# A bitonic sort beside graph layer 0: operand and mask of the compare-exchange held in PSUM

## The chip, the cores and the metric

The kernel runs on one core of a Trainium2 chip. The metric is the device time of one execution in microseconds. A core has TensorE (PE, with its weight loads PEld), VectorE (DVE), ScalarE (ACT), GpSimd (POOL) and SyncE (SP), which run side by side and wait for each other by semaphores. In this kernel POOL's main task is to issue gathers: DMAs that fetch 128 rows of a table by a list of indices.

## The reference

Four graph layers over 12500 nodes of 128 features and 200000 edges, each behind a layer norm with ReLU. Only layer 0 and the edge list of layer 1 bear on the change.

```python
edge_index = jnp.stack([src, dst])
h = jnp.maximum(_layernorm(x, axis=-1), 0.0)
x = x + _L0_gnn_ref(h, edge_index, edge_attr_64, ...)     # attention over incoming edges, sums by dst
h = jnp.maximum(_layernorm(x, axis=-1), 0.0)
x = x + _L1_gnn_ref(h, edge_attr_3, edge_weight1, ..., edge_index)   # attention, sums by src
...                                                        # layers 2 and 3

# layer 0
h = x @ W
a_s = h @ att_src
a_d = h @ att_dst
e = jax.nn.leaky_relu(a_s[src] + a_d[dst], NEG_SLOPE)
e = jnp.exp(e - seg_max[dst])
denom = jax.ops.segment_sum(e, dst, num_segments=N)
alpha = e / (denom[dst] + 1e-16)
out = jax.ops.segment_sum(h[src] * alpha[:, None], dst, num_segments=N)
```

Layer 0 sums over edges in the order of dst, in which the edges arrive. Layer 1 sums over edges in the order of src, so the kernel has to sort the edges by src first, and to carry edge_weight1 along.

## The kernel before, in words

**Layer 0's edges** (`layer0_edges`) go by in NW = 391 groups of G = 4 tiles of 128 edges. For each group POOL issues four gathers (line 289) that fetch 128 rows each of the table hw into the tile rows, of which there are eight buffers. SP loads a row of lanes. DVE turns lanes into a one-hot matrix (mine, L1116), PE multiplies it (pt, L1119), and DVE makes the edge weights from pt and the gathered rows (L1122 to L1130). ACT makes three of the four weight matrices (L1137, L1138), DVE the fourth (L1140). PE multiplies them by the rows (psum, L1143), and DVE adds the product to acc (L1146, two instructions per group).

**The sort** (`sort`, given out by `background`) runs in the same stretch of the program. After 8 of every 15 groups `layer0_edges` takes one step of it. The 200000 keys lie in a tile of 128 partitions with 13 x 128 elements each, and edge_weight1 in another of this shape, aux. A step is either a transposition of keys and aux (`turn`: PE multiplies by an identity or a diagonal matrix into the PSUM tile bank, of which there are two buffers, and ACT copies out; L459 to L470), or one compare-exchange of all pairs at a distance (`exchange`). Levels 1 to 6 treat the pairs in two pieces of 416 each, one upwards and one downwards, and the other levels mostly in one piece of 832 or 800. There are 171 exchanges with 194 pieces.

A piece has first operands a and second operands b, strided views of keys. Before the change:

- L427, DVE: mask = a > b (or a < b), into a contiguous SBUF tile mask
- L428, ACT: copies the first half of the pairs of aux into the SBUF tile swap
- L431 and L432, DVE: minimum and maximum of a and b into the other keys tile
- L437 and L438, DVE, once all pieces have had these: conditional copies within aux, the second half where mask is set into the first, and swap where mask is set into the second.

**Order.** The program is written in the order above; a scheduler of the framework then interleaves the instructions of groups and sort steps in each engine's queue, by its own costs. Each engine runs its queue in order. A tile with several buffers is written again when the readers of its last use are done.

Of the kernel before, what the change touches and what calls it, by code (L numbers as in the profile page):

```python
# [23 lines left out]
F32 = mybir.dt.float32  # L24
# [3 lines left out]
AF = mybir.ActivationFunctionType  # L28
# [8 lines left out]
P = 128  # L37
# [9 lines left out]
RC = -(-R // P)  # L47
# [57 lines left out]
class Net:  # L105
    def __init__(self, tc, a, out):
        self.tc, self.nc, self.a, self.out = tc, tc.nc, a, out

# [14 lines left out]

    def bank(self, psum):

        return psum.tile([P, 512], F32, name="bank", bufs=2)

    def constants(self, pool, temp, psum):  # L130
        nc, a = self.nc, self.a
# [263 lines left out]
    def sort(self, work, psum, keys, aux=None):  # L395

        nc = self.nc  # L400
        at, ax = 0, 0

        def flat(t):
            return t.rearrange("p c e -> p (c e)")

        def exchange(pieces, rest=(), both=True):


            nonlocal at
            k, o = flat(keys[at]), flat(keys[1 - at])  # L410
            if aux:
                mask = work.tile([P, RC * P // 2], F32, name="mask")
                swap = work.tile([P, RC * P // 2], F32, name="swap")
                v = flat(aux[ax])
            used = 0
            swaps = []
            for va, vb, up in pieces:
                a, b = va(k), vb(k)
                shape = list(a.shape[1:])
                n = int(np.prod(shape))  # L420
                if aux:
                    m, s = (t[:, used:used + n] for t in (mask, swap))
                    if len(shape) > 1:
                        names = "abc"[:len(shape)]
                        spec = f"p ({' '.join(names)}) -> p {' '.join(names)}"
                        m, s = (t.rearrange(spec, **dict(zip(names, shape))) for t in (m, s))
                    nc.vector.tensor_tensor(m, a, b, op=OP.is_gt if up else OP.is_lt)  # L427
                    nc.scalar.activation(s, va(v), AF.Copy)  # L428
                    swaps.append((va(v), vb(v), m, s))
                    used += n  # L430
                nc.vector.tensor_tensor(va(o), a, b, op=OP.min if up else OP.max)  # L431
                nc.vector.tensor_tensor(vb(o), a, b, op=OP.max if up else OP.min)  # L432
            for lo, hi in rest:
                nc.scalar.activation(o[:, lo:hi], k[:, lo:hi], AF.Copy)
            for a, b, m, s in swaps:
                m = m.bitcast(I32)
                nc.vector.copy_predicated(a, m, b)  # L437
                nc.vector.copy_predicated(b, m, s)  # L438
            at = 1 - at

        def halves(lo, hi, d):
            def view(h):
                return lambda t: t[:, lo:hi].rearrange("p (a h d) -> p a h d", h=2, d=d)[:, :, h, :]
            return view(0), view(1)

        def span(lo, n, to):
            return lambda t: t[:, lo:lo + n], lambda t: t[:, to:to + n]

        def turn(dst, src, level):

            for c0 in range(0, RC, 4):
                n = min(4, RC - c0)
                p = self.bank(psum).rearrange("p (c e) -> p c e", e=P)
                rows = P if c0 + n < RC else R - (RC - 1) * P
                for j in range(n):
                    c = c0 + j
                    cols = flat(src)[:, c * P:c * P + rows]
                    if level is None:
                        nc.tensor.transpose(p[:rows, j, :], cols, self.ident)  # L459
                    elif level == 0:  # L460
                        nc.tensor.transpose(p[:, j, :rows], src[:rows, c, :], self.ident[:rows, :rows])
                    else:
                        d = self.level_diag(c, level)
                        nc.tensor.matmul(p[:, j, :rows], src[:rows, c, :], d[:rows, :rows], start=True, stop=True)
                if level is None:
                    nc.scalar.activation(dst[:rows, c0:c0 + n, :], p[:rows, :n, :], AF.Copy)
                elif rows == P:
                    nc.scalar.activation(dst[:, c0:c0 + n, :], p[:, :n, :], AF.Copy)
                else:
                    nc.scalar.activation(flat(dst)[:, c0 * P:c0 * P + rows], p[:, 0, :rows], AF.Copy)  # L470

        def turn_all(level):
            nonlocal at, ax
            turn(keys[1 - at], keys[at], level)
            at = 1 - at
            if aux:
                turn(aux[1 - ax], aux[ax], None if level is None else 0)
                ax = 1 - ax


        for level in range(1, 8):
            for e in range(level - 1, -1, -1):
                d = 1 << e
                if level == 7:
                    exchange([(*halves(0, RC * P, d), True)])
                else:
                    size = 1 << level

                    def view(r, h, size=size, d=d):
                        return lambda t: t.rearrange("p (a r m h d) -> p a r m h d", r=2, m=size // (2 * d), h=2,  # L490
                                                     d=d)[:, :, r, :, h, :]
                    exchange([(view(0, 0), view(0, 1), False), (view(1, 0), view(1, 1), True)])
                yield None
        for level in range(8, 19):
            turn_all(level)
            yield None
            d = 1 << (level - 8)
            cols = R
            while d:
                if d < 64:  # L500
                    exchange([(*halves(0, cols, d), True)])
                elif d < 512:
                    exchange([(*halves(0, 24 * 64, d), True)], rest=[(24 * 64, cols)])
                elif d == 512:
                    exchange([(*span(0, 512, 512), True), (*span(1024, 64, 1536), True)], rest=[(1088, 1536)])
                else:
                    exchange([(*span(0, 576, 1024), True)], rest=[(576, 1024)])
                yield None
                d //= 2
            turn_all(None)  # L510
            yield None
            for e in range(6, -1, -1):
                exchange([(*halves(0, RC * P, 1 << e), True)])
                yield None
        yield keys[at], aux[ax] if aux else None
# [584 lines left out]
    def layer0_edges(self, acc, lists, tb, background):  # L1100
        nc, tc = self.nc, self.tc
        idx, place, half, mask, firsts = lists
        n = D + 2
        with tc.tile_pool(name="l02", bufs=1) as work, tc.tile_pool(name="ps02", bufs=2, space=PSUM) as psum:
            steps = background(psum)
            for g in range(NW):
                lo = g * G
# [13 lines left out]
                t = work.tile([P, G, 2, 3], F32, name="factor", bufs=2)  # L1121
# [19 lines left out]
                p = psum.tile([P, n], F32, name="psum", bufs=2)  # L1141
# [6 lines left out]
                    next(steps, None)  # L1148
            for _ in steps:
                pass  # L1150

    def layer0_wide(self, pool, acc, asd, least, wide, edges):

# [743 lines left out]
```

## Time and profile before

| | |
|---|---|
| median of 3 runs | 9236.6 us (9233.54 to 9252.93) |
| profiled execution, its own time | 9221.37 us |
| profiled execution, span from first to last instruction | 9219.6 us |
| first and last gather of hw | 177.5 and 2428.0 us from the span's start |
| busy in the span: PE, DVE, ACT, POOL | 6457.1, 6759.6, 4358.4, 5288.2 us |

The span is the time from the first instruction to the last. The profiled execution is 1.8 us longer than its span and 15.2 us shorter than the median of the runs. The busy time of an engine is the union of its instructions; a part of the kernel is read from its own stretch, not from these sums. In a group's row the number after the bar is the busy time, then the mean of one instruction in ns, then the engine's idle time just before them and what ended it.

### The profile page before, as it was taken

To read this page: it belongs to the slowest core of one execution; us is meant where nothing else is said; L and a number is where in the kernel's file an instruction comes from. 1 tells how busy PE (TensorE), PEld (TensorE's weight loads), DVE (VectorE), ACT (ScalarE), POOL (GpSimd) and SP (SyncE) were. 2 spreads that over 40 slices of the span, in tenths; PEclk is the share of its full clock that TensorE was granted. 3 is DMA by queue.
4 is the path that set the end of the run, shared out by engine and by line. 5 is a ranking of instruction groups with operands and counts; after the bars stand their busy time and mean duration, and the time that the engine had idled before them with its cause. 6 is when DMAs were issued, how large, how long until landed. Compare 5 with 4: busy or idle time off the path is not lost. (4 is left out here: it accounts for less than half of the span.)

```text
span 9219.6 us, 138919 instructions
## 1 busy us (share of the span) xinstructions
PE 6457.1 (70%) x35725; PEld 4629.3 (50%) x35726; DVE 6759.6 (73%) x24903; ACT 4358.4 (47%) x7941; POOL 5288.2 (57%) x5216
## 2 busy tenths in 40 slices
PE   4454545544456777777777638887888876999999
PEld 3344444444335777677667524444444433555555
DVE  5777677767656777877777787777777776777777
ACT  4444444444333555555565443333333335655555
POOL 1777777777535666567666457777777771000000
PEclk7555555555565555555555559999999997999999
DMA  4233333333464555455555413433444443233333
GB/s 111 72 71 71 69 71 72 70 70 71 129 190 145 166 163 162 139 155 162 159 161 161 121 56 111 117 114 109 116 117 117 112 121 101 87 99 97 98 97 111
DMA packets 916156, 1046.92 MB, mean 114 GB/s; under 512 B 136970, under 2 KB 754595, under 8 KB 914593
## 3 DMA queue, kind: packets, MB, share of 16 engines
q1 hardware_dynamic: 698837, 557.92, 21.7%
q0 software_dynamic: 185408, 438.42, 17.4%
q10 hardware_dynamic: 31115, 41.46, 1.5%
q8 instruction: 319, 5.23, 0.2%
q14 instruction: 477, 3.90, 0.1%
HBM read 977.06 MB, written 86.50 MB: 115 GB/s over the span
## 5 line engine op out<-in xcount | busy, mean ns | idle before, releaser
L849 PE MATMUL sums<-yours,r 128*128 128x482 f16 x10192 | 2535.5, 373 | 192.8 <-ACT r L875 149.5
L875 ACT ACTIVATE r<-pout 128x512 f16<-128x512 f32 x2548 | 1480.0, 596 | 1940.4 <-PE pout L870 1914.2
L289 POOL DMA_INDIRECT rows<-hw,idxd x1564 | 1773.0, 1134 | 653.4 <-issue 390.0
L289 POOL DMA_INDIRECT rows<-kvt,idxs x1660 | 1600.0, 964 | 852.0 <-issue 399.0
L872 DVE TENSOR_SCALAR yours<-iotac,bucketp 128x482 f16<-128x482 f16 x5096 | 1642.1, 358 | 387.2 <-PE sums L849 386.5
L289 POOL DMA_INDIRECT rows<-zt,idxs x1660 | 1614.8, 973 | 509.9 <-issue 403.5
L849 PEld LDWEIGHTS <-r 128*128 128x128 f16 x10192 | 970.7, 99 | 988.7 <-ACT r L875 349.4
L1143 PE MATMUL psum<-rows,weights 128*128 128x130 f32 x3128 | 812.1, 435 | 703.5 <-ACT weights L1138 651.0
L1143 PEld LDWEIGHTS psum<-rows,weights 128*128 128x128 f32 x3128 | 690.1, 321 | 785.4 <-ACT weights L1138 744.3
L1317 PE MATMUL psum<-weighted,hot 128*128 128x137 f32 x3320 | 843.6, 432 | 252.1 <-DVE lg L1294 93.0
L870 PE MATMUL pout<-z,mine 128*128 128x256 f16 x5096 | 928.3, 277 | 11.1 <-DVE mine L864 8.9
L1317 PEld LDWEIGHTS psum<-weighted,hot 128*128 128x128 f32 x3320 | 741.0, 316 | 302.1 <-ACT weighted L1307 144.5
L1138 ACT ACTIVATE weights<-off,weight,minus 128x128 f32<-128x128 bf16 x1173 | 496.8, 482 | 833.3 <-DVE rows L1130 741.3
L1463 DVE TENSOR_TENSOR acc<-acc,psum 128x128 f32 x1660 | 464.6, 280 | 488.3 <-PE psum L1459 482.9
L1289 PE MATMUL pb<-we,near 128*128 128x8 f32 x3320 | 688.5, 336 | 165.1 <-PE psum L1317 91.7
L1289 PEld LDWEIGHTS pb<-we,near 128*128 128x128 f32 x3320 | 683.5, 304 | 222.4 <-PE psum L1317 128.3
L1286 ACT ACT_TABLE_LOAD x370 | 474.7, 1283 | 638.5 <-DMA near<-lengths 635.5
L870 PEld LDWEIGHTS <-mine 128*128 128x128 f16 x5096 | 479.1, 98 | 452.5 <-DVE mine L864 51.1
L1319 DVE TENSOR_TENSOR acc<-acc,psum 128x137 f32 x1660 | 488.5, 294 | 225.7 <-PE psum L1317 218.5
L1282 PE MATMUL pq<-q,mine 128*128 x3320 | 460.3, 286 | 230.1 <-DVE mine L1278 122.4
L1307 ACT ACT_TABLE_LOAD x370 | 474.7, 1283 | 309.9 <-DVE lg L1302 269.9
L1282 PEld LDWEIGHTS <-mine 128*128 128x128 f16 x3320 | 368.6, 133 | 286.2 <-issue 123.0
(455 smaller groups left out, 9490.8 us busy)
## 6 DMA issues: line engine op xcount, KB each, us to landing
lanes<-lanes SPq DMA_DIRECT2D x168, 896.0 KB
near<-lengths SPq DMA_DIRECT2D x415, 256.0 KB
lanes<-slanes SPq DMA_DIRECT2D x415, 128.0 KB
lanes<-dlanes SPq DMA_DIRECT2D x391, 128.0 KB
z<-zt SPq DMA_DIRECT2D x98, 448.0 KB
z<-h SPq DMA_DIRECT2D x98, 448.0 KB
rows<-kvt,idxs POOLq DMA_INDIRECT x1660
rows<-zt,idxs POOLq DMA_INDIRECT x1660
```

The source lines that it names most:

```text
L289: self.nc.gpsimd.indirect_dma_start(out=out, out_offset=None, in_=table, in_offset=bass.IndirectOffsetOnAxis(ap=idx[:, t:t + 1], axis=0))
L849: nc.tensor.matmul(sums[i], self.part(r[:, i, :], h), yours[:, i, :], start=s == 0 and h == 0, stop=s == NB - 1 and h == PARTS - 1)
L870: nc.tensor.matmul(p[:, j, :], mine[:, (i + j) * P:(i + j + 1) * P], z[:, s % ZB, :], start=True, stop=True)
L872: nc.vector.tensor_scalar(yours[:, j, :], self.iotac, place[:, b:b + 1], None, op0=OP.is_equal)
L875: nc.scalar.activation(r, p, AF.Copy)
L1138: nc.scalar.activation(hot[:, j, :], off, AF.Relu, bias=w[:, j:j + 1], scale=minus[:, j:j + 1])
L1143: nc.tensor.matmul(p, hot[:, j, :], rows[:, j, :n], start=j == 0, stop=j == G - 1)
L1282: nc.tensor.matmul(pq[:, j, :], mine[:, j, :], q[:, bass.ds(blocks[j], 1), h, :].rearrange("p a d -> p (a d)"), start=h == 0, stop=h == 1)
L1286: nc.scalar.activation(hid, hid, AF.Silu, bias=self.be1, scale=self.we1)
L1289: nc.tensor.matmul(pb[:, j, :], hid[:, j, :], self.we2, start=True, stop=True)
L1317: nc.tensor.matmul(p, hot, v[:, j, :], start=True, stop=True)
L1319: nc.vector.tensor_add(d, d, p)
```

## The change

In an exchange that carries aux, the mask is no longer a tile in SBUF. mask and a new tile first are the two buffers of bank in PSUM. ScalarE copies the first operand a of each piece into first, in contiguous order, and DVE reads first wherever it read a: for the comparison, the minimum and the maximum. The conditional copies read the mask from PSUM. The second operand b, aux and swap stay in SBUF. For the length of `layer0_edges` a buffer of bank is two PSUM banks wide (1024 elements of fp32), so that a piece of 832 fits; `turn` uses the first 512 elements of it.

```diff
@@ class Net, __init__
+        self.banks = 1
@@ def bank(self, psum)
-        return psum.tile([P, 512], F32, name="bank", bufs=2)
+        return psum.tile([P, 512 * self.banks], F32, name="bank", bufs=2)
@@ def sort, exchange
             if aux:
-                mask = work.tile([P, RC * P // 2], F32, name="mask")
+                mask, first = self.bank(psum), self.bank(psum)
                 swap = work.tile([P, RC * P // 2], F32, name="swap")
                 v = flat(aux[ax])
...
                 if aux:
-                    m, s = (t[:, used:used + n] for t in (mask, swap))
+                    m, s, f = (t[:, used:used + n] for t in (mask, swap, first))
                     if len(shape) > 1:
...
-                        m, s = (t.rearrange(spec, **dict(zip(names, shape))) for t in (m, s))
+                        m, s, f = (t.rearrange(spec, **dict(zip(names, shape))) for t in (m, s, f))
+                    nc.scalar.activation(f, a, AF.Copy)
+                    a = f
                     nc.vector.tensor_tensor(m, a, b, op=OP.is_gt if up else OP.is_lt)
                     nc.scalar.activation(s, va(v), AF.Copy)
@@ def sort, turn
-                p = self.bank(psum).rearrange("p (c e) -> p c e", e=P)
+                p = self.bank(psum)[:, :512].rearrange("p (c e) -> p c e", e=P)
@@ def layer0_edges
+            self.banks = 2
             steps = background(psum)
...
             for _ in steps:
                 pass
+            self.banks = 1
```

The sort before layer 0, which runs only where the edges do not come in order, carries no aux and is left as it is.

## The prediction

> **What bounds the kernel now.** I read the page first, for where the sort beside layer 0 lies: the slices in which POOL shows 7 and DVE 5 to 8, from 177 to 2428 us. Then the busy time of each engine in that stretch, the groups of POOL, and the waits.
>
> ```profile
> 177.00:2428.00 2251.00, 1093.46 (x5398) 938.68 (x5397) 1590.84 (x4910) 1056.63 (x2728) 1773.16 (x1565) 0.55 0.31 73
> ```
>
> ```profile
> L289 POOL DMA_INDIRECT rows<-hw,idxd x1564 | 1773.0, 1134 | 653.4 <-issue 390.0 <-ACT off L1137 176.0 <-DMA rows<-hw,idxd 34.3
> ```
>
> The first view's columns are PE, PEld, DVE, ACT, POOL. No engine looks full; POOL comes nearest with 1773 of 2251 us. The group's row tells why it is the bound all the same: of its idle time 176 us lie before the first gather. Read one by one, the 1564 gathers run from 177.5 to 2428.0 us with a gap of 0.303 to 0.306 us between each two of nearly all (477.6 us in 1563 gaps; two exceed 0.4 us). POOL never stands for a buffer. So the stage lasts as long as the gathers: 1773 + 478 = 2251 us.
>
> The waits of this stretch show the others following:
>
> ```profile
> DVE weight L1125 <- DMA rows<-hw,idxd: 350.0, 175, 10.4
> ACT swap L428 <- DVE aux L438: 207.2, 78, 8.4
> ...
> DVE factor L1122 <- PE pt L1119: 143.6, 162, 2.0
> DVE acc L1146 <- PE psum L1143: 111.9, 155, 1.4
> ```
>
> DVE stands 350 us until gathered rows land. The other large DVE waits, 143.6 + 111.9 = 255 us, are for PE.
>
> Next, why a gather takes 1134 ns on average. Half of them take 940 to 945 ns, the longest 2597. The timeline shows which are long:
>
> ```profile
> 1005.64 1.01 DVE L427 TENSOR_TENSOR mask<-keys 128x832 f32<-128x832 f32 x1
> ...
> 1005.83 1.64 POOL L289 DMA_INDIRECT rows<-hw,idxd  x1 [0.30 <-issue]
> ...
> 1017.24 1.01 DVE L431 TENSOR_TENSOR keys<-keys 128x832 f32<-128x832 f32 x1
> 1017.31 1.76 POOL L289 DMA_INDIRECT rows<-hw,idxd  x1 [0.30 <-issue]
> ```
>
> A gather that starts while a sort instruction runs ends 0.82 us after that instruction ends (1006.65 + 0.82 = 1007.47; 1018.25 + 0.82 = 1019.07). It is held until the instruction is done. Counted over all gathers against 944 ns: 296.5 us too long in all. 284 us of it are on gathers that overlap a sort instruction (L427, L431, L432, L437, L438); 12 us belong to the packing of the keys and the like, which the change leaves.
>
> [...] The trace agrees, by a pair in layer 1 of equal size:
>
> ```profile
> 3601.21 0.69 DVE L1310 TENSOR_TENSOR weighted<-rows,weighted 128x512 f32<-128x512 f32 x1
> ...
> 3601.46 1.25 POOL L289 DMA_INDIRECT rows<-kvt,idxs  x1 [1.88 <-DVE weighted L1310]
> ...
> 3604.22 0.68 DVE L1291 TENSOR_TENSOR rows<-pq,rows 128x512 f32<-128x512 f32 x1
> 3604.27 0.95 POOL L289 DMA_INDIRECT rows<-kvt,idxs  x1 [0.30 <-issue]
> ```
>
> L1310 reads two SBUF tiles; L1291 reads pq from PSUM and rows from SBUF. Of the gathers that start inside L1310 and beside nothing else, 73 of 73 exceed 1000 ns (mean 1241); inside L1291, 0 of 117 (mean 945).
>
> [...] The same pair says less: 687 ns with PSUM (L1291), 685 without (L1310). The measurement decides; I take 0[...].
>
> [...]
>
> **The change part by part.**
>
> (1) L427, L431 and L432 read their first operand from PSUM: one SBUF input each, as L1291. From the gathers that start inside one of them alone: L427 109 gathers of mean 1403, L431 101 of 1345, L432 84 of 1457; against 944 that is 50 + 40 + 43 = 133 us gone from POOL. This half has a precedent in the trace. Duration as now (901 ns mean over all forms)[...].
>
> (2) L437 and L438 read the mask from PSUM. One input (aux or swap) stays in SBUF. Gathers that start inside L437: 104 of mean 1621, inside L438: 108 of 1593; 70 + 70 = 140 us. No copy with a mask in PSUM is in the trace. Upper end: all 140 us go[...]. Lower end: none, if the conditional copy reads its destination too, which would be a second SBUF input. I take all. The sum of (1) and (2), 273 us, reaches 284 us with the gathers that overlap two of these instructions.
> Its duration has two values by access pattern: the 832-element copy takes 1.02 to 1.16 us, but 2.0 us at distances of one and two elements (mean 1.33). With the mask elsewhere the slow form may vanish (DVE gains about 100 us) or stay; I take that it stays, which costs nothing against now.
>
> (3) Added: 194 ScalarE copies of the first operand into PSUM. The nearest row is L428, the same sizes into SBUF: 194 x 0.80 = 156 us. ACT goes from 1057 to 1213 us, 62% of a stage of 1966 us. PSUM as target may be somewhat faster[...].
>
> (4) Added waits. L427 now waits for that copy. Behind it in DVE's queue stand the group's instructions, and PE, ACT and the release of rows wait on those. In the queue order of the changed kernel, between L432 of one exchange and L427 of the next stand the two conditional copies (2 us and more) and group work, so the copy is mostly covered: 0 to 0.8 us per exchange, I take 0.4 x 171 exchanges = 68 us of DVE idle. On ACT the copy stands ahead of activations that make PE's weights; it waits for L432, which comes before the L438 that L428 waits for already.
>
> (5) mask and first take both buffers of bank, in PSUM. A transposition of the keys, which now may start after L432, must wait for L438: two copies, 2 to 4 us, at 22 places (11 levels, twice); 44 to 88 us on the sort's own chain, in part beside group work. The swap copies already wait for L438.
>
> (6) Outside the stage the instructions are the same. In the layer 1 table that follows, some change places in the queues: 0, with 5 us either way.
>
> **Is POOL still the bound?** Gathers: 1564 x (0.944 + 0.305) = 1953 us, and 12 us left over: about 1966. DVE: 1591 busy + 255 for PE + 68 for the copy = 1914. It fits, tightly. One stretch does not: the first 21 exchanges run in two pieces of 416. Each is 6 x 0.60 + 4 x 0.89 = 7.2 us of DVE; fifteen groups hold eight: 57 us, with 15 x 1.52 us of group work ((1591 - 995) / 391) and 10 us for PE that is 90 us against 75 of gathers. Over some 39 groups this falls 39 us behind; eight rows buffers cover some 25. I charge 15 us of waiting POOL there and 10 us for the transpositions.
>
> Sum: -284 + 25 = -259 us. The profiled execution took 9221.4 us (span 9219.6), so 8962; the median of the runs is 15 us higher, 9236.6, so **8978**.
>
> **Rivals.**
> - The conditional copies still hold the gathers. For: their half-rate form at small distances, which L431 with the same patterns does not have[...]. Against: at larger distances they run[...] as L431 does[...]. Then only (1) counts: -133 us, and up to 25 given back: 9104 to 9128.
> - DVE's queue becomes the bound: waits for the copy and the transpositions sum to 150 us or more. Stage 2000 to 2100: 9090 at -150.
> - Slower: the copy in ACT's queue closes a ring. It waits for L432 behind it the weights, PE waits for the weights, DVE's L1146 for PE, and L427 for the copy. The gathers lose their lead of eight buffers, and DVE sets the time: 1591 + 255 + 171 x w. This passes 2251 at w = 2.4 us per exchange; at 3 us it is 2359, +108: 9345. For: L428 already stands 2.7 us on average (207.2 / 78) at 78 places. Against: DVE hardly ever waits for ACT today.
> - No change: the holding of the gathers is another one's doing. L1291 against L1310 speaks against it.
>
> **How the numbers follow.** As reckoned (gain of 200 to 300 us): 0.72. Copies still hold: 0.14. DVE's queue: 0.06. No change: 0.03. Slower: 0.05. About 0.2% (18 us) is what a measurement can tell from no change. Faster 0.92, same 0.03, slower 0.05. The lower end is all 297 us gone, 8940, less 5 for the spread of runs; the upper end takes in most of the copies' case, 9115.
>
> **What would show it.** Gathers of hw at a mean of 950 ns for 1134, the last near 2165 us for 2428; DVE's wait for ACT's copy under 100 us; POOL's wait for rows under 40. Gathers that start inside L437 or L438 and still end 0.82 us after it would prove the first rival; gaps on POOL above 0.31 us with DVE over 90% busy, the second; a gather mean of 950 and a stage over 2251 us, the third.

## The result and the profile after

| | before | after |
|---|---|---|
| median | 9242.23 us (4 runs, 9233.54 to 9252.93) | 8986.18 us (4 runs, 8973.02 to 8987.83) |
| profiled execution: span | 9219.6 us | 8971.1 us |
| first and last gather of hw | 177.5 and 2428.0 us | 177.2 and 2150.6 us |

The ratio is 0.9719, with a 95% interval of 0.9702 to 0.9736: 256 us less. The forecast was 8978 us, with a range of 8935 to 9115. In the kernel after, the new ScalarE copy is L429, the comparison L431, the swap copy L432, minimum and maximum are L435 and L436, the conditional copies L441 and L442, and a gather is L290.

First the group of hw gathers in the view by lines of the kernel after (busy time, mean in ns of one, idle time before them and its causes):

```profile
L290 POOL DMA_INDIRECT rows<-hw,idxd x1564 | 1491.9, 954 | 657.3 <-issue 398.9 <-ACT off L1142 175.8 <-PE psum L1148 31.6
```

1491.9 for 1773.0 us, at a mean of 954 ns for 1134. The idle time is what it was (657.3 for 653.4): 176 us ahead of the first gather, and 481.5 us in the 1563 gaps, of which only four exceed 0.4 us. By the same reading as before, POOL is still the bound. The view of busy time in the stretch from the first gather to the last (columns PE, PEld, DVE, ACT, POOL):

```profile
177.00:2150.60 1973.60, 1038.81 (x5373) 888.38 (x5373) 1585.22 (x4880) 1187.39 (x2905) 1491.88 (x1564) 0.57 0.38 83
```

The stretch is 277 us shorter. DVE's work in it is the same (1585 us for 1591), so it is now busy for 80% of it, for 71% before; ACT for 60%, for 47%.

The timeline of the kernel after (start, duration, engine, line) shows gathers that start inside three of the sort's instructions:

```profile
1003.71 0.99 DVE L431 TENSOR_TENSOR bank<-bank,keys 128x800 f32<-128x800 f32 x1
...
1004.14 0.94 POOL L290 DMA_INDIRECT rows<-hw,idxd  x1 [0.30 <-issue]
...
1004.87 0.98 DVE L435 TENSOR_TENSOR keys<-bank,keys 128x800 f32<-128x800 f32 x1
1005.39 0.94 POOL L290 DMA_INDIRECT rows<-hw,idxd  x1 [0.30 <-issue]
...
1006.78 0.84 ACT L429 ACTIVATE bank<-keys 128x800 f32<-128x800 f32 x1 [1.73 <-DVE keys L436]
1007.56 0.35 DVE L1151 SCALAR_TENSOR_TENSOR acc<-psum,mask,acc 128x130 f32 x1
1007.82 0.99 DVE L442 COPY_PREDICATED aux<-bank,swap 128x800 f32<-128x800 int32 x1
1007.88 0.94 POOL L290 DMA_INDIRECT rows<-hw,idxd  x1 [0.30 <-issue]
...
1009.05 1.00 DVE L431 TENSOR_TENSOR bank<-bank,keys 128x800 f32<-128x800 f32 x1
```

Each of the three gathers takes 0.94 us. Over the stage, the gathers that start inside L431, L435, L436, L441 or L442 number 112, 118, 101, 136 and 152. Here and below, as in the prediction's counts, a gather is counted as starting inside an instruction when it starts at least 0.02 us after that instruction's start and at least 0.2 us before its end; it may run on into the next instruction. Their means are 944 to 945 ns and none exceeds 1000; before, the means were 1403, 1345, 1457, 1621 and 1593. It is the start that decides: before the change, 350 gathers started outside the five sort instructions and had one of them start while they ran, and only 9 of these exceed 1000 ns. Of the 296.5 us above 944 ns apiece, 15.5 are left, mostly beside the packing. The fence also shows where the new copy goes: L429 runs from 1006.78 to 1007.62, beside DVE's conditional copies, and is done 1.4 us before L431 needs it.

The waits of the stage after (us in total, times, longest):

```profile
DVE acc L1151 <- PE psum L1148: 144.4, 213, 3.3
DVE factor L1127 <- PE pt L1124: 135.8, 173, 1.9
ACT bank L429 <- DVE keys L436: 125.8, 72, 4.9
...
ACT swap L432 <- DVE aux L442: 96.6, 69, 3.1
...
DVE weight L1130 <- DMA rows<-hw,idxd: 45.0, 19, 5.6
...
POOL rows L290 <- PE psum L1148: 31.6, 96, 1.8
```

The wait for gathered rows fell from 350.0 to 45.0 us: DVE's slack was in that wait, and the faster gathers took it up. The other row that DVE and PE decide is POOL's: 31.6 us over 96 gaps is 0.33 us each, hardly more than the ordinary gap of 0.30.

### The profile page after: what moved, and what is told of

Same layout as the page of the kernel before. It is cut to its first block, busy times and chain, and to the rows that moved or that the text cites. A ratio compares the mean times of both kernels' runs of the same rounds, so it can differ in the third digit from the quotient of the medians.

```text
span 8971.1 us, 139090 instructions
## 1 busy us (share of the span) xinstructions
PE 6429.0 (72%) x35725; PEld 4599.1 (51%) x35726; DVE 6762.6 (75%) x24903; ACT 4491.0 (50%) x8133; POOL 5017.4 (56%) x5216
## 3 DMA queue, kind: packets, MB, share of 16 engines
q0 software_dynamic: 185408, 438.42, 18.6%
## 5 line engine op out<-in xcount | busy, mean ns | idle before, releaser
L290 POOL DMA_INDIRECT rows<-kvt,idxs x1660 | 1604.5, 967 | 863.2 <-issue 401.2
L290 POOL DMA_INDIRECT rows<-zt,idxs x1660 | 1619.3, 975 | 509.8 <-issue 425.9
L290 POOL DMA_INDIRECT rows<-hw,idxd x1564 | 1491.9, 954 | 657.3 <-issue 398.9
L1148 PE MATMUL psum<-rows,weights 128*128 128x130 f32 x3128 | 769.6, 417 | 596.8 <-ACT weights L1143 519.9
L1148 PEld LDWEIGHTS psum<-rows,weights 128*128 128x128 f32 x3128 | 654.7, 305 | 677.1 <-ACT weights L1143 598.7
```

The source lines that it names most:

```text
L290: self.nc.gpsimd.indirect_dma_start(out=out, out_offset=None, in_=table, in_offset=bass.IndirectOffsetOnAxis(ap=idx[:, t:t + 1], axis=0))
L1148: nc.tensor.matmul(p, hot[:, j, :], rows[:, j, :n], start=j == 0, stop=j == G - 1)
```

## The experiments

The first four ran on a chip on which the kernel before has a median of 9242.08 us (15 runs, 9224.07 to 9253.14), the time of the first measurement (9242.23 us); both are called the first chip here. The other eight ran on two other chips, on which both kernels take over 10300 us.

### Only the first operand in PSUM

```diff
-                mask, first = self.bank(psum), self.bank(psum)
+                mask, first = work.tile([P, RC * P // 2], F32, name="mask"), self.bank(psum)
```

> First operand in PSUM, mask in SBUF as before. Theory A (a DVE instruction with two SBUF inputs holds back the gather that starts beside it): the gathers that start inside the comparison, minimum and maximum are free (944 ns), those that start inside the conditional copies are still held (about 1600 ns). The sum of the gathers is about 1773 - 133 = 1640 us and the kernel 120 to 150 us faster than before, about 9105. Rival B (the gain comes from the ScalarE copy, which makes the first operand contiguous, and the other order of the queues, not from where the operand lies): the whole 256 us. Rival C (only the conditional copies matter): nothing.

Measured: 9116.13 us (9098.17 to 9125.16), ratio 0.9858 (0.9840 to 0.9875), 126 us less than before. Its view by lines has the gathers at

```profile
L290 POOL DMA_INDIRECT rows<-hw,idxd x1564 | 1646.6, 1053 | 653.3 <-issue 384.8 <-ACT off L1142 177.1 <-PE psum L1148 29.2
```

that is 126 us less than the 1773.0 before. Its timeline:

```profile
1003.21 2.00 DVE L442 COPY_PREDICATED aux<-mask,swap 128x832 f32<-128x832 int32 x1
...
1003.71 2.12 POOL L290 DMA_INDIRECT rows<-hw,idxd  x1 [0.30 <-issue]
...
1007.96 1.02 DVE L431 TENSOR_TENSOR mask<-bank,keys 128x832 f32<-128x832 f32 x1
...
1008.63 0.94 POOL L290 DMA_INDIRECT rows<-hw,idxd  x1 [0.31 <-issue]
```

The gather inside the conditional copy with its mask in SBUF is held, until 0.62 us after its end; the one inside the comparison is free. Over the stage, the 312 that start inside L431, L435 or L436 average 943 to 944 ns, the 115 inside L441 1634 and the 110 inside L442 1551. The first operand gives half of the gain, by the instructions that read it and by no others.

### Only the mask in PSUM

```diff
-                mask, first = self.bank(psum), self.bank(psum)
+                mask = first = self.bank(psum)
...
-                    nc.scalar.activation(f, a, AF.Copy)
-                    a = f
```

The copy is gone; first is only another name for the mask's tile, and no instruction uses it. The comparison is here L429, minimum and maximum L433 and L434, the conditional copies L439 and L440.

> Mask in PSUM, first operand read from SBUF as before, no ScalarE copy. Theory A: gathers that start inside the conditional copies are free, those inside comparison, minimum and maximum are held; the comparison writes PSUM and still reads two SBUF tiles. The sum of the gathers is about 1773 - 140 = 1633 us, kernel 125 to 155 us faster, about 9100. If a conditional copy reads its destination through the second input too: nothing gained. Rival B: nothing gained. The conditional copy at distances 1 and 2 stays at 2.0 us, as in the changed kernel.

Measured: 9108.84 us (9098.04 to 9118.80), ratio 0.9848 (0.9831 to 0.9864), 133 us less. View by lines and timeline of this kernel:

```profile
L290 POOL DMA_INDIRECT rows<-hw,idxd x1564 | 1641.1, 1049 | 654.9 <-issue 393.6 <-ACT off L1140 175.7 <-DMA rows<-hw,idxd 32.3
```

```profile
1001.98 2.01 DVE L440 COPY_PREDICATED aux<-bank,swap 128x832 f32<-128x832 int32 x1
...
1003.18 0.94 POOL L290 DMA_INDIRECT rows<-hw,idxd  x1 [0.30 <-issue]
...
1006.81 1.03 DVE L429 TENSOR_TENSOR bank<-keys 128x832 f32<-128x832 f32 x1
...
1006.93 1.71 POOL L290 DMA_INDIRECT rows<-hw,idxd  x1 [0.30 <-issue]
```

Now it is the other way round: 283 gathers start inside L439 or L440, at 943 to 944 ns; those inside L429, L433 and L434 take 1420, 1402 and 1456. The comparison also writes to PSUM here, and holds the gather all the same: its two inputs decide. This settles the rival that the conditional copies would go on holding: a conditional copy that reads its mask from PSUM does not hold a gather, although it writes into part of a tile in SBUF. The two halves sum to 126 + 133 = 259 us, and the whole change measured 256.

### Everything of the change but the place of the tiles

```diff
-                mask, first = self.bank(psum), self.bank(psum)
+                mask, first = (work.tile([P, RC * P // 2], F32, name=i) for i in ("mask", "first"))
```

The ScalarE copy and DVE's wait for it stay, with both tiles in SBUF. (The transpositions then don't share buffers with them.)

> The ScalarE copy and its wait as in the changed kernel, but first and mask both in SBUF. Theory A: all five sort instructions have two SBUF inputs again, the gathers are held as before (sum about 1773 us), so the time is that of before, 9225 to 9260, a few us more at most for the copy. Rival B: about 8986, as the changed kernel.

Measured: 9252.80 us (12 runs, 9244.68 to 9261.05), ratio 1.0012 (1.0003 to 1.0020), 11 us more than before. View by lines and timeline of this kernel:

```profile
L290 POOL DMA_INDIRECT rows<-hw,idxd x1564 | 1779.1, 1138 | 652.3 <-issue 388.5 <-ACT off L1142 175.1 <-DMA rows<-hw,idxd 34.2
```

```profile
1010.51 1.01 DVE L431 TENSOR_TENSOR mask<-first,keys 128x832 f32<-128x832 f32 x1
...
1010.69 1.64 POOL L290 DMA_INDIRECT rows<-hw,idxd  x1 [0.30 <-issue]
```

All five hold again (1396, 1344, 1522, 1611 and 1639 ns on average for gathers that start inside L431, L435, L436, L441 and L442). The copies, the waits and the order in the queues are worth nothing or a little less than nothing; the gain is the place of the operands.

### The kernel before, once more

No edit; one run, for the spread between executions.

> The kernel before once more, for a second profile. It tells how much the stages behind layer 0 differ between two executions of one program. In the pair of profiles layer 1's gathers took 2497 us before and 2511 after the change, with the same instructions. If that is the spread of executions, this one may lie anywhere within 15 us of 2497; if it comes from the changed kernel, this one is within 3 us of 2497. The gathers of hw end at 2428 us within 2.

Measured: 9262.61 us, gathers at

```profile
L289 POOL DMA_INDIRECT rows<-hw,idxd x1564 | 1784.9, 1141 | 652.0 <-issue 387.8 <-ACT off L1137 174.4 <-DMA rows<-hw,idxd 35.5
```

and the last one at 2438.6 us, 11 us later than in the first profile. The gathers' time above 944 ns apiece is 308.5 us here for 296.5: how long they are held varies between executions, so a single profile of a kernel with held gathers is good to some 10 us, not to 2 as was expected. Layer 1's stretch of gathers took 2509.9 us here and 2496.9 in the first profile; in the profiles of the kernel after and of the three variants above it took 2511.3, 2513.0, 2506.4 and 2504.4.

### The kernel after on two other chips

No edit.

> The changed kernel once more, beside the next three on the same chip. About 8986, within 10; its layer 1 gathers anywhere from 2497 to 2513 us, as in the five profiles so far. This run is what the next three are measured against.

> The changed kernel again. On the chip of the last four runs the kernel before took 10492 us and the changed one 10526: there GpSimd stood 980 us between its gathers (481 in the first profile), and DVE, ACT and PE stood for instructions with no releaser that the profile knows. If this chip is like the first (before near 9242), the changed kernel is at about 8986 and GpSimd's gaps sum to 480 us. If the change itself has such an unstable state, before is at 9242 and this kernel is not at 8986.

Measured, second chip: kernel before 10492.44 us (53 runs, 10465.72 to 10536.86), kernel after 10526.26 (10509.90 to 10539.35), ratio 1.0037 (1.0024 to 1.0049). Third chip: before 10344.16 (63 runs, 10312.49 to 10380.83), after 10371.20 (10347.20 to 10406.69), ratio 1.0023 (1.0013 to 1.0033). The 8986 us that both expectations name did not come: on these chips the kernel before is slower too, and the gain is gone. The reason is not that the gathers are held. The page of the kernel after on the second chip:

```profile
L290 POOL DMA_INDIRECT rows<-hw,idxd x1564 | 1487.7, 951 | 1155.2 <-issue 418.0
```

The mean is 951 ns, as on the first chip. But the idle time is 1155 us for 657, 979 of it in the gaps, and the last gather comes at 2644.4 us (third chip: 2594.8). DVE's busy time from 177 to 2645 us is 1592 us, as before: it has no more work. Its waits from 178 to 2650 us:

```profile
PEld psum L1148 <- issue: 305.5, 114, 17.9
POOL rows L290 <- PE psum L1148: 284.6, 89, 9.9
...
DVE acc L1151 <- remote: 237.9, 67, 19.3
PE psum L1148 <- issue: 208.3, 57, 17.6
DVE factor L1127 <- remote: 188.6, 39, 9.5
```

"issue" and "remote" mean that this core's records name no releaser. L1127 and L1151 are the two DVE instructions that take results from PE, and POOL waits for L1148 to release rows. PE itself stands there with nothing to wait for that the profile shows: 305.5 us over 114 waits of its weight loads, where the kernel after on the first chip has 32.5 us over 13. So as far as the waits show, PE's late instructions hold up the stage on these chips, and faster gathers end in a wait. Why PE is late was not found: in this stage the granted clock is 0.55 on the second chip and 0.57 on the first, too near for a stage 494 us longer (2467 us for 1973), and the packets of the gathers take 147 and 164 ns each on average, so they are not slower there. The other stages are longer there too: layer 1's gathers take 3099 and 3051 us in the kernel after, for 2511. No profile of the kernel before was taken on these chips, so that the same wait bounds it there is likely, not shown.

### The index constant for the sort's end made early

```diff
@@ constants
+        self.thr = pool.tile([P, NB], F32, name="thr")
+        nc.gpsimd.iota(self.thr, pattern=[[P, NB]], base=0, channel_multiplier=0,
+                       allow_small_or_imprecise_dtypes=True)
@@ items
-        thr = pool.tile([P, NB], F32, name="thr")
-        nc.gpsimd.iota(thr, pattern=[[P, NB]], base=0, channel_multiplier=0, allow_small_or_imprecise_dtypes=True)
+        thr = self.thr
```

This was aimed at the end of the stage, shown below.

> The changed kernel, with the tile of thresholds thr made by GpSimd at the program's start instead of where the list for layer 1 begins. In the changed kernel that instruction stands behind all gathers of layer 0 (2150.6 us), and VectorE stands 11.2 us for it with the last groups' work behind; in the kernel before it ran 31 us ahead of the last gather. If the wait delays the end of layer 0, the step from the last gather of hw to edge_i falls from 20.6 to about 14 us and the kernel gains 5 to 8 us. If something else is last there (the store of the keys, the last groups), it gains nothing.

> As thr_early, where GpSimd is the bound: 5 to 8 us faster than the changed kernel if VectorE's 11 us behind thr delay the end of layer 0 (from the last gather of hw to edge_i 14 us for 20.6), else no difference.

Measured: 10507.57 us on the second chip, ratio 1.0024 (1.0015 to 1.0034); 10363.01 us on the third, 1.0019 (1.0009 to 1.0029). Against the kernel after that is 19 and 8 us less, with intervals that overlap. From the last gather of hw to the gather of edge_i it took 18.6 and 17.9 us, where the kernel after took 20.8 and 20.5 on these chips. That is 2 to 3 us of the step. The kernel of the next section says the same: there the scheduler has put the constant 24 gathers ahead of the last one, and the step is 17.6 and 17.4 us. On a chip where POOL sets the stage it was not tried.

### The ScalarE copy issued twice

```diff
                     nc.scalar.activation(f, a, AF.Copy)
+                    nc.scalar.activation(f, a, AF.Copy)
                     a = f
```

> The changed kernel with each ScalarE copy of the first operand made twice: 194 more activations, about 156 us more ScalarE time, and the comparison waits 0.8 us longer for its operand. If the copy is covered by other work and GpSimd stays the bound, 0 to 15 us slower than the changed kernel. If the ring ScalarE to VectorE to ScalarE is near the bound, 0.8 x 171 = 137 us slower or more.

> As copy_twice, where GpSimd is the bound: 0 to 15 us slower than the changed kernel if the copy is covered, 137 us or more if the ring of ScalarE and VectorE is near the bound.

Measured: 10510.17 us, ratio 1.0017 (1.0006 to 1.0027); 10375.06 us, 1.0026 (1.0016 to 1.0036). Against the kernel after -16 and +4 us. 194 more copies cost nothing that can be told, so no ring through ACT's queue (the prediction's slower rival) is near. This holds for chips on which ACT has more time in the stage (1192 of 2468 us busy) than on the first (1187 of 1974); there it was not tried.

### Four row buffers for eight

```diff
-                rows = work.tile([P, G, ROW], F32, name="rows", bufs=8)
+                rows = work.tile([P, G, ROW], F32, name="rows", bufs=4)
```

This asks whether the lead of the gathers covers the two-piece exchanges.

> The changed kernel with four buffers of gathered rows instead of eight. In the first 250 us the two-piece exchanges make VectorE the slower one: the sort reaches its first transposition 12 us earlier than before, while gathers run about 50 us ahead, so some 38 us of lead are used up. Eight buffers hold 40 us of gathers, four hold 20. If that lead is what keeps GpSimd from waiting, GpSimd waits 15 to 25 us early in layer 0 and the kernel is 10 to 25 us slower than the changed kernel. If the lead is not needed, the same time.

> As rows4, where GpSimd is the bound: GpSimd waits 15 to 25 us early in layer 0 and the kernel is 10 to 25 us slower than the changed kernel if the lead of eight buffers is used up by the two-piece exchanges; no difference if it is not needed.

Measured: 10480.16 us (10461.00 to 10505.40), ratio 0.9994 (0.9985 to 1.0003); 10330.72 us (10301.16 to 10354.07), 0.9989 (0.9977 to 1.0001). It is 46 and 40 us faster than the kernel after on the same chips, on both with intervals that do not overlap, and within about 0.1% of the kernel before. That was not expected, and what brings it is open. To the question it gives no answer: it was tried only where POOL stands 911 to 944 us between its gathers anyway.

## Why the prediction was right

**The bound** was read rightly on the first chip: the gathers sum up to the stage, before and after (1491.9 + 481.5 = 1973.4 us).

**The hold** of the gathers was read rightly. For the other direction, a DVE instruction that waits for a running gather, the profiles show none. Before the change, 58 comparisons of 832 elements start while a gather runs; they take 1017 ns on average, as do the 26 that start between gathers, and DVE stands 0.0 to 0.7 us in all before each of the five sort instructions. So nothing was there for DVE to gain. A held gather ends 0.82 us after a comparison, minimum or maximum, as read in the prediction; after the two conditional copies it is less, 0.64 and 0.78 us (medians).

**(1) First operand, forecast -133.** By itself it gave -126. DVE did not pay for it: L431, L435 and L436 take 176.4 + 174.2 + 174.2 = 524.8 us in all, for 524.4 before, 902 and 901 ns each.

**(2) Mask, forecast -140.** By itself it gave -133, so the choice of the upper end was right. It was the author's estimate, since no copy with a mask in PSUM was in the trace. That the 2.0 us form of the conditional copies stays was right too: L441 and L442 sum to 467.9 us for 468.2.

**(3) ACT, forecast +156.** The copies take 151.4 us, 780 ns each. Copying the same operands into SBUF (the third experiment) took 156.5 us, 816 ns each, so PSUM as target was somewhat faster here, by 36 ns.

**(4) The wait for the copy, forecast 68 us: missed.** The groups of DVE and ACT after:

```profile
L431 DVE TENSOR_TENSOR bank<-bank,keys 128x832 f32<-128x832 f32 (+4 forms) x194 | 176.4, 909 | 2.6 <-ACT bank L429 1.1
L429 ACT ACTIVATE bank<-keys 128x832 f32<-128x832 f32 (+4 forms) x194 | 151.4, 780 | 128.5 <-DVE keys L436 125.8
```

DVE stands 1.1 us for it in all. The failed step is the middle value of 0.4 us per exchange, taken between two ends although the queue order that the prediction itself names (two conditional copies and group work in between) covers the copy nearly everywhere.

**(5) Transpositions, forecast 44 to 88 us of the sort's chain: missed.** All instructions on the bank tiles together had only 8.0 us of idle time, at 9 places, that ended with L442.

**The charges of +15 and +10 us** were too high. POOL's gaps above 0.4 us sum to 6.4 us. DVE did fall behind, but less than reckoned: the sort reached its first transposition at 550.1 us, 12 us earlier than before, while the gathers were 36 us ahead of before there (the 292nd starts at 551 us, for 587). That uses about 23 us of lead, not the 39 of the prediction (nor the 38 that the expectation for four buffers names). The eight buffers, put at 25 us there, just covered it: POOL waited for one twice, 1.8 us at 501 us and 1.2 us at 527 us. So the stage gained 277 us instead of 259.

**(6) Outside the stage, forecast 0 ± 5: missed, the other way.** Of the 277.4 us by which the last gather came earlier, 270.9 were left when the gather of edge_i started, and 248.5 at the end of the span. The end of the stage, first in the kernel before, then after:

```profile
2435.68 0.74 DVE L1146 SCALAR_TENSOR_TENSOR acc<-psum,mask,acc 128x130 f32 x2 [0.89 <-PE psum L1143]
...
2442.07 0.97 POOL L289 DMA_INDIRECT edge_i<-sown,ri  x1 [12.81 <-DVE ri L544]
```

```profile
2149.66 0.94 POOL L290 DMA_INDIRECT rows<-hw,idxd  x1 [0.30 <-issue]
2150.61 0.26 POOL L536 IOTA thr<- 128x98 f32 x1
...
2150.91 1.49 DVE L538 TENSOR_TENSOR lt<-firsts,thr 128x1274 f32<-128x1274 f32 x1 [11.21 <-POOL thr L536]
...
2164.05 0.74 DVE L1151 SCALAR_TENSOR_TENSOR acc<-psum,mask,acc 128x130 f32 x2 [1.43 <-PE psum L1148]
...
2171.16 0.97 POOL L290 DMA_INDIRECT edge_i<-sown,ri  x1 [19.14 <-DVE ri L548]
```

The gather of edge_i follows the last gather of hw by 20.5 us, for 14.0 before. In between lies the work of the last groups: their last product goes into acc 14.2 us after the last gather, for 8.4 before. Two things lie in it. The constant thr, which the sort's end needs, now stands behind the last gather in POOL's queue, and DVE stands 11.2 us for it with the last groups' work queued behind; before, it stood 24 gathers ahead. By the runs on the other two chips it is worth 2 to 3 us. And more is left to do: when the last gather ends, the last products of five groups are still to come, for three before. The kernel with four row buffers has two left there, and a step of 15.8 and 14.8 us although the constant stands behind its last gather. On the first chip the two were not separated.

The other 22 us lie behind that, 14 of them in layer 1's gathers (2511 us for 2497 in the first profile of before). Since a second execution of the unchanged kernel has them 13 us longer too, this is put down to the spread between executions, not to the change.

That the total came so near is luck in part. Stage and rest err in opposite directions, by 18 us and by about 20, so the gain is 256 us for the 259 forecast; the rest of the 8 us is the median of before, 9236.6 us when the forecast was made and 9242.2 with a fourth run.

**The rivals.** "The copies still hold" fell with the second experiment. "DVE's queue" and the ring through ACT did not come on the first chip: DVE is busy for 80% of the stage, and its wait for the copy is 1.1 us. "No change" fell with the third experiment. What no rival foresaw is that on other chips the gathers are not the bound of the changed kernel: there the change costs 0.2 to 0.4%.

## What to carry to other kernels

A gather that POOL issues was held by every kind of large two-input VectorE instruction looked at here (comparison, minimum, maximum, product, conditional copy) when both inputs lay in SBUF: the gathers that start inside took 1241 to 1621 ns on average in the kernel before. When one lay in PSUM they took 943 to 945. If POOL's queue sets a stage, put one of the two inputs into PSUM, and let an engine with time to spare carry it there. Look for it by sorting POOL's instructions by what VectorE runs when they start: a mean over all hides it. Before counting on the gain, see that nothing else is just below the bound, and measure on more than one chip: here the same edit gave 2.8% on one and nothing on two others.

## What the hardware showed beyond that

- For a conditional copy the place of the mask decided, with data and destination in SBUF both times: with the mask in SBUF too, the gathers that start inside take 1634 and 1551 ns on average (only the first operand in PSUM); with the mask in PSUM, 943 to 944 ns, and 0 of 283 are held. So the destination did not count as a second input.
- The 2.0 us form of the conditional copy (1.04 us otherwise, for 832 elements) comes at distances of one and two elements, for L442, whose data and mask are contiguous, as well as for L441. Minimum and maximum with a destination strided in the same way take 1.02 us. What the slow copies have in common is the conditional write into runs of one or two elements; why it takes longer was not shown. The place of the mask changes nothing in it: 47 of the 194 copies of each line have it before and after, at a mean of 1.97 to 1.98 us.
- Two inputs are not the only case. In the kernel after, L1121 compares one bf16 tile in SBUF (128x512) with one number per partition, in 359 ns. Of the 47 gathers that start inside it, 28 exceed 1000 ns. The gathers that start beside it are 3.9 us of the 15.5 us that are left.
- The comparison that writes to PSUM and reads SBUF twice holds a gather as long as before (1420 ns on average, for 1403); where the result goes did not matter.
- The kernel before took 9242 us on one chip and 10344 and 10492 us on two others, 12 and 14% more. Its granted clock is 0.72 to 0.73 on the first and 0.70 to 0.71 on the others, some 3% apart.
